# Layer 0's bias keys in the score products: two products of 260 columns in place of one of 512 and a separate path

## The chip, the cores and the metric

The kernel runs on one core of a Trainium2 chip. Its time is the device time of one execution in microseconds; the lower, the better. TensorE is called PE here, VectorE DVE, ScalarE ACT, GpSimd POOL, and SP is the engine that issues the DMAs. PEld is the loading of stationary weights into PE.

## The reference

The reference is a stack of four cross-attention layers on x (4 batches of 512 tokens, 512 wide) with a context of 64 tokens in each batch. The change is in layer 0. It has two attentions, one after the other, with 16 heads of 128 columns and one learned bias key and bias value for each head, and then an MLP. In short:

```python
h = layer_norm(x, ln_scale, ln_offset)
qh = (h @ wq + bq).reshape(b, 512, 16, 128)
kh = (ctx @ wk + bk).reshape(b, 64, 16, 128)
kh = concat([kh, broadcast(bias_k)], axis=1)        # 65 keys for each head
vh = concat([vh, broadcast(bias_v)], axis=1)
w = softmax(einsum("bqhk,bthk->bhqt", qh, kh) / sqrt(128))
x = x + einsum("bhqt,bthk->bqhk", w, vh).reshape(b, 512, 2048) @ wo + bo
```

Each query row has 65 scores for each head: 64 of the context, and one of the bias key. The bias key is the same in all batches. Everything is in fp32.

## The kernel before

**Algebra.** The kernel never forms the queries. `l0_project` multiplies each head's key matrix by its query weights once: `A[c]` (c is one of NC = 4 blocks of 128 rows of the model width) holds wq times the keys of a head, so that scores are h times A. `cq` holds what the query bias adds. `U` holds values times output weights. A head's row in `A` and `cq` is KW = 260 columns: 4 batches of 64 keys, and then four equal columns for the bias key. The keys of a head come into the tile `kT`: an evacuation from PSUM that adds the key bias (`shift`, on ACT or DVE) writes 256 columns, and a small POOL copy (L718) writes the bias key into the last four. L729 is the product for A (260 columns), L735 that for cq, L748 and L761 those for U and the bias values.

**Loops.** Each of the two attentions (n) does its 16 heads in two halves of HH = 8. For each half, `l0_project` is called, and then `l0_attention` for each of the 4 batches b. Inside, t goes over NT = 4 tiles of 128 query rows. So there are 16 calls of `l0_attention` and 64 tiles. The normalised input, transposed, is `hT` (transposes L675, evacuated with scale and offset at L496 or L497).

**A call of `l0_attention` before the change.** First the scores of the bias keys for all 512 rows: four products (L793), each with 32 columns of `A[c]` as the stationary side, taken with a step of 65 through its 8 rows, and `hT[c]` as the moving side; each writes its own 32 partitions of one bank. The result is copied to SBUF (`sbT`). Four small products with `fold` (L802) add up the four blocks and turn the result around, and a DVE add (L807) with a column of cq gives `last`: for each row of each tile, the 8 scores of the bias keys. Then for each tile:

- the scores of the context: `mm4` (L634), four accumulating products of 512 columns (8 heads of 64) into one PSUM bank `p`
- DVE adds cq (L825) into `s3`, 8 heads of 65, and copies the 8 scores of `last` (L827) into the 65th places
- maximum (L830), subtraction (L832), exp on ACT (L834), sum (L837), reciprocal (L839)
- POOL multiplies by the reciprocal (L842, L844), PE transposes (L853), DVE or ACT copies
- the output product `mm4` with U (L634 too), and a DVE add into x (L861).

L634 is the line of the helper `mm4`; all its users stand under it, and the shapes tell them apart. L926 is the product of the MLPs, which take up most of the kernel after layer 0's attention; L885 is their additions on DVE or POOL.

**Order.** The order is not written by hand. Each `with pe(...)`, `dve(...)`, `either(...)` records an operation with an assumed cost. `Plan.order` then plays the program through with those costs, engine by engine: an engine takes the earliest recorded operation whose inputs are there and whose buffers fit, within a distance `AHEAD`. So operations of several tiles and of the next projection lie between one another. The result is a fixed order on each engine; waits are semaphores. PSUM is `Memory(1024, 4)`: four blocks of two banks (512 fp32 columns each), which can be split; `ps()` takes one bank, `ps(2)` a block. A tile's buffer comes free in the plan when its last user is done.

Of the kernel before, what the change touches and what calls it, by code (L numbers as in the profile page):

```python
# [14 lines left out]
ALU = mybir.AluOpType  # L15
# [3 lines left out]
P = 128  # L19
B = 4  # L20
S = 512
D = 512
T = 64
NT = S // P
NC = D // P
H = 16
HH = H // 2
DH = 32
KW = B * T + 4
F = 2048  # L30
LOWEST = -3.4028234663852886e38

# [164 lines left out]
class Plan:  # L197
# [19 lines left out]
    def sb(self, n):  # L217
        return Buf(self.sbuf, n)

    def ps(self, banks=1):  # L220
        return Buf(self.psum, 512 * banks)
# [308 lines left out]
def t_dve(n):  # L530
    return 0.15 + n * 0.00105


def t_act(n):
    return 0.19 + n * 0.00083
# [5 lines left out]

MM = {512: 0.859, KW: 0.438, 256: 0.432}
TR = 0.109
ROWS = 1.08
# [14 lines left out]
def stack(nc, const, sbuf, psum, a, out):  # L559
# [6 lines left out]
    fold = const.tile([P, P], FP, name="fold")  # L566
# [27 lines left out]
    sb, ps = pl.sb, pl.ps  # L594

    def col(name, i=None):
        lo, hi = _COL_AT[name]
        return cols[:, lo:hi] if i is None else cols[:, lo + i : lo + i + 1]


    def pe(us):
        return pl.op(PE=us)

    def dve(n):
        return pl.op(DVE=t_dve(n))
# [4 lines left out]
    def pool(n):  # L610
        return pl.op(POOL=t_pool(n))

    def either(n):
        return pl.op(ACT=t_act(n), DVE=t_dve(n))
# [5 lines left out]
    def loaded(src, *sizes):  # L620

        n = math.prod(sizes)
        t = sb(n)
        load(t.v(*sizes), src, n)
        return t

    def chunks(w):

        return w.rearrange("(c p) n -> p c n", p=P)

    def mm4(o, dst, lhs, rhs):

        for c in range(NC):
            o.matmul(dst, lhs(c), rhs(c), start=(c == 0), stop=(c == NC - 1))  # L634
# [53 lines left out]
    def l0_project(n, half):  # L688
        A = [sb(HH * KW) for _ in range(NC)]
        cq = sb(HH * KW)  # L690
        U = [sb(HH // 2 * D) for _ in range(B)]
        if not half:

            bvd = sb(H * DH)
            with pool(512) as o:
                o.memset(bvd.v(), 0.0)
            for g in range(4):
                with pool(4) as o:
                    o.tensor_copy(
                        bvd[:, g * 129 : g * 129 + 109 : 36], col(f"L0_xattn_bias_v{n}")[:, 4 * g : 4 * g + 4]  # L700
                    )
            bias[n] = [bvd, sb(D), None]
        bvd, ub, _ = bias[n]
        vTs, wos = [], []
        for j in range(HH):
            h = half * HH + j
            heads = slice(h * P, (h + 1) * P)

            wk = loaded(chunks(a[f"L0_wk{n}"][:, heads]), NC, P)
            wq = loaded(a[f"L0_wqT{n}"][heads, :], D)  # L710
            kT = sb(KW)
            p = ps()
            with pe(4 * MM[256]) as o:
                mm4(o, p[:, : B * T], lambda c: wk.v(NC, P)[:, c, :], lambda c: ctxT[:, c, :])
            with either(256) as o:
                o.shift(kT[:, : B * T].k(0), p[:, : B * T], col(f"L0_xattn_bk{n}", h))
            with pool(1) as o:
                o.tensor_copy(kT[:, B * T :].k(1), col(f"L0_xattn_bias_k{n}", h).to_broadcast([P, 4]))  # L718
            wv = loaded(chunks(a[f"L0_wv{n}"][:, heads]), NC, P)
            vT = sb(B * T)  # L720
            p = ps()
            with pe(4 * MM[256]) as o:
                mm4(o, p[:, : B * T], lambda c: wv.v(NC, P)[:, c, :], lambda c: ctxT[:, c, :])
            with either(256) as o:
                o.shift(vT.v(), p[:, : B * T], col(f"L0_xattn_bv{n}", h))
            for c in range(NC):
                p = ps()
                with pe(MM[KW]) as o:
                    o.matmul(p[:, :KW], wq[:, c * P : (c + 1) * P], kT.v(), start=True, stop=True)  # L729
                with either(KW) as o:  # L730
                    o.move(A[c].v(HH, KW)[:, j, :].k(j), p[:, :KW])

            p = ps()
            with pe(MM[KW]) as o:
                o.matmul(  # L735
                    p[:, :KW], col(f"L0_xattn_bq{n}", h).to_broadcast([P, P]), kT.v(), start=True, stop=True
                )
            with either(KW) as o:
                o.move(cq.v(HH, KW)[:, j, :].k(j), p[:, :KW])
            wo = loaded(a[f"L0_wo{n}"][heads, :], D)  # L740
            vTs.append(vT)
            wos.append(wo)
            if j % 2:
                for b in range(B):
                    p = ps()
                    with pe(PAIR) as o:
                        for e in range(2):
                            o.matmul(  # L748
                                p[e * T : (e + 1) * T, :],
                                vTs[j - 1 + e][:, b * T : (b + 1) * T],  # L750
                                wos[j - 1 + e].v(),
                                start=True,
                                stop=True,
                            )
                    with either(D) as o:
                        o.move(U[b].v(HH // 2, D)[:, j // 2, :].k(j // 2), p.v())
            if j % 4 == 3:
                p = ps()
                with pe(ROWS) as o:
                    for i in range(4):  # L760
                        o.matmul(  # L761
                            p[i * DH : (i + 1) * DH, :],
                            bvd.v(H, DH)[:, h - 3 + i, :],
                            wos[j - 3 + i].v(),
                            start=True,
                            stop=True,
                        )
                if h == 3:
                    with either(D) as o:
                        o.move(ub.v(), p.v())  # L770
                else:
                    with dve(D) as o:
                        o.tensor_tensor(ub.v(), p.v(), ub.v(), ALU.add)
        if half:

            ubr = sb(D)
            p = ps()
            with pe(MM[512]) as o:
                o.matmul(p.v(), fold, ub.v(), start=True, stop=True)
            with either(D) as o:  # L780
                o.move(ubr.v(), p.v())
            bias[n][2] = ubr
        return A, cq, U

    def l0_attention(n, half, b, hT, proj, pb):
        qs = 1.0 / math.sqrt(P)
        A, cq, U = proj


        p = ps()  # L790
        with pe(ROWS) as o:
            for c in range(NC):
                o.matmul(  # L793
                    p[c * DH : (c + 1) * DH, :], A[c][:, KW // 4 - 1 :: KW // 4], hT[c].v(), start=True, stop=True
                )
        sbT = sb(S)
        with either(S) as o:
            o.move(sbT.v(), p.v())
        p = ps()
        with pe(8 * TR) as o:  # L800
            for t in range(NT):
                o.matmul(  # L802
                    p[:, t * HH : (t + 1) * HH], sbT[:, t * P : (t + 1) * P], fold[:, 3:DH:4], start=True, stop=True
                )
        last = sb(NT * HH)
        with dve(32) as o:
            o.tensor_tensor(  # L807
                last.v(NT, HH),
                p[:, : NT * HH].split(NT, HH),
                cq.v(HH, KW)[:, :, B * T].new(1).bc(P, NT, HH),  # L810
                ALU.add,
            )
        for t in range(NT):
            p = ps()
            with pe(4 * MM[512]) as o:
                mm4(
                    o,
                    p.v(HH, T),
                    lambda c: hT[c][:, t * P : (t + 1) * P],
                    lambda c: A[c].v(HH, KW)[:, :, b * T : (b + 1) * T],  # L820
                )
            sc = sb(HH * (T + 1))
            s3 = sc.v(HH, T + 1)
            with dve(512) as o:
                o.tensor_tensor(s3[:, :, :T].k(0), p.v(HH, T), cq.v(HH, KW)[:, :, b * T : (b + 1) * T], ALU.add)  # L825
            with dve(8) as o:
                o.tensor_copy(s3[:, :, T].k(1), last.v(NT, HH)[:, t, :])  # L827
            m = sb(HH)
            with dve(520) as o:
                o.tensor_reduce(m.v(), s3, AX.X, ALU.max)  # L830
# [19 lines left out]
            p = ps()  # L850
# [6 lines left out]
            p = ps()  # L857
# [4 lines left out]
        if half:  # L862

            p = ps()
# [643 lines left out]
    for n in (1, 2):  # L1508
        hT, pb = [], []
# [16 lines left out]
    h = {}  # L1526
# [106 lines left out]
```

## Time and profile before

| | |
|---|---|
| median of 3 runs | 2876.68 us (2876.4 to 2878.92) |
| profiled execution | 2877.63 us |
| its span, first to last instruction | 2875.8 us |
| mean granted PE clock | 0.993 |
| PE busy | 2799.8 us, 97% of the span |
| DVE busy | 1841.8 us, 64% |
| ACT busy, POOL busy | 812.1 us (28%), 903.8 us (31%) |
| DMA | 129.58 MB, 45 GB/s in the mean |
| first product of an MLP (L926) | 810.11 us from the start |

The profile is of one execution. Matmuls are pipelined, and the ends of their records are modelled, so "busy" of PE is the time that some matmul record covers. The mean of a group is how long one record lasted, not how far apart two of them are. Each fp32 product of the program is two records on PE, and two weight loads. A group of instructions shows the line, the engine, the tiles written and read, the count, busy time, the mean of one in ns, and the idle time of the engine just before, with what ended it.

### The profile page before, as it was taken

The numbers are of one execution on the slowest core, as the hardware profiler recorded it, in microseconds if no ns is written. First come the engines' busy times: TensorE is split into PE (matmuls) and PEld (weight loads), VectorE is DVE, ScalarE is ACT, GpSimd is POOL, SyncE is SP. The second block draws the span as 40 slices with busy tenths as digits, with TensorE's granted clock in tenths as the row PEclk, the third lists the DMA queues.
The fourth block names the chain that finished last, engine by engine and source line by source line (L and its number), as shares of the span: only waits on it lengthen the run. The fifth ranks groups of instructions, "written<-read, shape, count | busy, mean of one in ns | idle before, by whom it ended". The sixth has DMA issues, their size and how long they took to land. (4 is left out here: it accounts for less than half of the span.)

```text
span 2875.8 us, 29017 instructions
## 1 busy us (share of the span) xinstructions
PE 2799.8 (97%) x10284; PEld 1421.3 (49%) x10284; DVE 1841.8 (64%) x3207; ACT 812.1 (28%) x1472; POOL 903.8 (31%) x847
## 2 busy tenths in 40 slices
PE   8999999999999999999999999999999998999999
PEld 6456455465455444454545445444444443444444
DVE  5646655555754475765667667476776677667655
ACT  1210111201231113543453345155432314232211
POOL 2530222501441251123113112212444456344531
PEclk9999999999999999999999999999999999999999
DMA  5112021120111220011112001201101020112110
GB/s 165 34 40 78 2 79 34 36 79 3 33 55 44 62 66 23 12 47 39 30 37 77 1 23 37 74 16 30 59 30 44 30 88 15 38 36 74 59 44 29
DMA packets 131023, 129.58 MB, mean 45 GB/s; under 512 B 6800, under 2 KB 105744, under 8 KB 130880
## 3 DMA queue, kind: packets, MB, share of 16 engines
q1 hardware_dynamic: 130512, 127.43, 14.1%
q8 instruction: 82, 1.34, 0.2%
q14 instruction: 61, 0.50, 0.1%
q0 software_dynamic: 80, 0.16, 0.0%
q10 hardware_dynamic: 288, 0.15, 0.0%
HBM read 123.52 MB, written 4.19 MB: 44 GB/s over the span
## 5 line engine op out<-in xcount | busy, mean ns | idle before, releaser
L926 PE MATMUL banks<-arena 128*128 128x512 f32 x2688 | 1213.7, 598 | 19.7 <-ACT arena L1336 6.8
L634 PE MATMUL banks<-arena 128*128 128x512 f32 (+2 forms) x1968 | 825.7, 570 | 1.3 <-ACT arena L487 1.0
L926 PEld LDWEIGHTS banks<-arena 128*128 128x128 f32 x2688 | 499.0, 191 | 618.3 <-issue 534.4
L885 POOL TENSOR_TENSOR arena<-arena 128x512 f32<-128x512 f32 x292 | 420.9, 1448 | 656.4 <-DVE arena L488 184.9
L634 PEld LDWEIGHTS banks<-arena 128*128 128x128 f32 x1968 | 358.6, 190 | 418.1 <-issue 395.4
L488 DVE COPY arena<-banks 128x512 f32<-128x512 f32 (+3 forms) x538 | 313.9, 589 | 184.4 <-PE banks L926 64.7
L487 ACT COPY arena<-banks 128x512 f32<-128x512 f32 (+3 forms) x370 | 192.9, 542 | 576.0 <-PE banks L926 185.3
L885 DVE TENSOR_TENSOR arena<-arena 128x512 f32<-128x512 f32 x320 | 310.9, 980 | 65.4 <-ACT arena L960 22.4
L960 ACT ACTIVATE arena<-arena,cols 128x512 f32<-128x512 f32 x192 | 137.8, 721 | 452.6 <-DVE arena L885 218.3
L945 DVE TENSOR_TENSOR arena<-banks,arena 128x512 f32<-128x512 f32 x240 | 164.4, 687 | 122.2 <-PE banks L926 113.7
L1336 ACT ACTIVATE arena<-banks,arena 128x512 f32<-128x512 f32 x256 | 174.5, 687 | 118.6 <-DVE arena L1326 63.7
L842 POOL TENSOR_TENSOR arena<-arena 128x512 f32<-128x512 f32 x64 | 71.5, 1117 | 416.8 <-DVE arena L839 381.4
L1324 DVE TENSOR_REDUCE arena<-banks 128x1 f32<-128x512 f32 x256 | 168.0, 682 | 12.5 <-PE banks L1313 11.6
L493 DVE TENSOR_SCALAR arena<-banks,cols 128x256 f32<-128x256 f32 (+1 forms) x103 | 59.6, 579 | 171.5 <-PE banks L634 166.2
L634 PE MATMUL banks<-ctxT,arena 128*128 128x256 f32 x640 | 150.5, 386 | 10.1 <-DMA arena<-in_L_wk 7.7
L1370 PEld LDWEIGHTS banks<-ident,arena 128*128 128x128 f32 x1024 | 119.5, 144 | 81.0 <-ACT arena L1336 33.9
L1370 PE MATMUL banks<-ident,arena 128*128 128x128 f32 x1024 | 140.2, 281 | 10.2 <-ACT arena L1336 8.8
L634 PEld LDWEIGHTS banks<-ctxT,arena 128*128 128x128 f32 x640 | 120.7, 192 | 44.0 <-issue 13.2
L984 DVE TENSOR_TENSOR arena<-banks,arena 128x512 f32<-128x512 f32 x144 | 98.5, 687 | 67.2 <-PE banks L926 66.8
L834 ACT ACTIVATE arena<-arena 128x520 f32<-128x520 f32 x64 | 40.8, 637 | 325.5 <-DVE arena L832 319.7
L1347 POOL TENSOR_TENSOR arena<-arena 128x256 f32<-128x256 f32 x64 | 40.2, 628 | 285.8 <-DVE arena L1326 171.3
L666 POOL TENSOR_SCALAR arena<-arena 128x512 f32<-128x512 f32 x48 | 100.5, 2101 | 48.3 <-DVE arena L661 34.7
(147 smaller groups left out, 2369.8 us busy)
## 6 DMA issues: line engine op xcount, KB each, us to landing
arena<-in_L_w SPq DMA_DIRECT2D x192, 256.0 KB, 3.7
arena<-in_L_wk SPq DMA_DIRECT2D x48, 256.0 KB, 3.3
arena<-in_L_wqT SPq DMA_DIRECT2D x32, 256.0 KB, 4.3
arena<-in_L_wv SPq DMA_DIRECT2D x32, 256.0 KB, 4.4
arena<-in_L_wo SPq DMA_DIRECT2D x32, 256.0 KB, 3.5
arena<-in_L_wo SPq DMA_DIRECT2D x8, 1024.0 KB, 5.4
arena<-in_L_wv SPq DMA_DIRECT2D x6, 1024.0 KB, 8.6
arena<-in_L_wq SPq DMA_DIRECT2D x5, 1024.0 KB, 8.5
```

The lines of the kernel that those rows point to most:

```text
L487: "ACT": lambda e, out, in_: e.copy(out, in_),
L488: "DVE": lambda e, out, in_: e.tensor_copy(out, in_),
L634: o.matmul(dst, lhs(c), rhs(c), start=(c == 0), stop=(c == NC - 1))
L666: o.tensor_scalar(n.v(), src[t].v(), mv.v(NT, 2)[:, t, 0:1], rstd[:, t : t + 1], ALU.subtract, ALU.mult)
L885: o.tensor_tensor(out, x, y, op)
L926: o.matmul(p.v(), lhs(c, m), rhs(c), start=(c == 0), stop=(c == 1))
L945: o.tensor_tensor(t.v(), p.v(), y.v(), ALU.add)
L960: o.activation(g[f].v(), src.v(), func, bias=col(b1, q * NC + f))
L984: o.tensor_tensor(r.v(), p.v(), r.v(), ALU.add)
L1324: o.tensor_reduce(m[:, i : i + 1].k(i), banks[i].v(), AX.X, ALU.max)
L1336: o.activation(y.v(), banks[i].v(), AF.Exp, bias=nm[:, i : i + 1].k(i), scale=qs, accum_out=sums[:, i : i + 1].k(i),)
L1370: o.transpose(p[:, c * P : (c + 1) * P], e[i][:, c * P : (c + 1) * P], ident)
```

## The change

A head's row stays at KW = 260 columns, but is laid out as 4 batches of 65: 64 keys and the bias key as the 65th. The shift into `kT` writes four runs of 64 with a step of 65, and the POOL copy writes the 65th columns. In `l0_attention` the path of the bias keys (L793, `sbT`, L802, L807, L827) is gone. The scores of a tile have 8 x 65 = 520 columns, which is more than one bank of 512. They are made by two `mm4` of 260 columns, four heads each, into the two banks of a `ps(2)`; the stationary blocks of `hT` are loaded for each of the two. One DVE add takes all 520 columns from both banks.

```diff
-KW = B * T + 4
+KW = B * (T + 1)
...
-                o.shift(kT[:, : B * T].k(0), p[:, : B * T], col(f"L0_xattn_bk{n}", h))
+                o.shift(kT.v(B, T + 1)[:, :, :T].k(0), p[:, : B * T].split(B, T), col(f"L0_xattn_bk{n}", h))
             with pool(1) as o:
-                o.tensor_copy(kT[:, B * T :].k(1), col(f"L0_xattn_bias_k{n}", h).to_broadcast([P, 4]))
+                o.tensor_copy(kT.v(B, T + 1)[:, :, T].k(1), col(f"L0_xattn_bias_k{n}", h).to_broadcast([P, B]))
...
-        p = ps()
-        with pe(ROWS) as o:
-            for c in range(NC):
-                o.matmul(
-                    p[c * DH : (c + 1) * DH, :], A[c][:, KW // 4 - 1 :: KW // 4], hT[c].v(), start=True, stop=True
-                )
-        sbT = sb(S)
-        with either(S) as o:
-            o.move(sbT.v(), p.v())
-        p = ps()
-        with pe(8 * TR) as o:
-            for t in range(NT):
-                o.matmul(
-                    p[:, t * HH : (t + 1) * HH], sbT[:, t * P : (t + 1) * P], fold[:, 3:DH:4], start=True, stop=True
-                )
-        last = sb(NT * HH)
-        with dve(32) as o:
-            o.tensor_tensor(
-                last.v(NT, HH),
-                p[:, : NT * HH].split(NT, HH),
-                cq.v(HH, KW)[:, :, B * T].new(1).bc(P, NT, HH),
-                ALU.add,
-            )
         for t in range(NT):
-            p = ps()
-            with pe(4 * MM[512]) as o:
-                mm4(
-                    o,
-                    p.v(HH, T),
-                    lambda c: hT[c][:, t * P : (t + 1) * P],
-                    lambda c: A[c].v(HH, KW)[:, :, b * T : (b + 1) * T],
-                )
+            p = ps(2)
+            own = slice(b * (T + 1), (b + 1) * (T + 1))
+            with pe(8 * MM[KW]) as o:
+                for i in range(2):
+                    mm4(
+                        o,
+                        p.v(2, 512)[:, i, :KW],
+                        lambda c: hT[c][:, t * P : (t + 1) * P],
+                        lambda c: A[c].v(HH, KW)[:, 4 * i : 4 * i + 4, own],
+                    )
             sc = sb(HH * (T + 1))
             s3 = sc.v(HH, T + 1)
-            with dve(512) as o:
-                o.tensor_tensor(s3[:, :, :T].k(0), p.v(HH, T), cq.v(HH, KW)[:, :, b * T : (b + 1) * T], ALU.add)
-            with dve(8) as o:
-                o.tensor_copy(s3[:, :, T].k(1), last.v(NT, HH)[:, t, :])
+            with dve(520) as o:
+                o.tensor_tensor(
+                    sc.v(2, 4, T + 1),
+                    p.v(2, 512)[:, :, :KW].arrange("p i (h s) -> p i h s", h=4),
+                    cq.v(2, 4, KW)[:, :, :, own],
+                    ALU.add,
+                )
```

## The prediction

> **What bounds the kernel now.** I read the page's first two parts, then busy time by window, the groups by shape, and last the order of PE in time, with the start of each run of matmuls. The page's busy times first:
>
> ```profile
> PE 2799.8 (97%) x10284; PEld 1421.3 (49%) x10284; DVE 1841.8 (64%) x3207; ACT 812.1 (28%) x1472; POOL 903.8 (31%) x847
> ```
>
> PE is the only engine near full, but this is an average over stages, so I ask for the stage of the change. Layer 0's attention runs from about 76 us, and the first product of the MLP after it (L926) starts at 810.11 us. Windows in it (us; busy time of PE, PEld, DVE, ACT, POOL):
>
> ```profile
> 100.00:175.00 75.00, 75.00 (x258) 37.84 (x256) 42.96 (x82) 18.14 (x28) 37.51 (x35) 1.00 0.03 8
> 270.00:330.00 60.00, 60.00 (x201) 27.81 (x194) 34.59 (x66) 9.00 (x15) 10.97 (x16) 1.00 0.00 1
> 475.00:525.00 50.00, 47.37 (x162) 23.89 (x161) 32.23 (x68) 15.72 (x24) 33.30 (x38) 1.00 0.00 1
> 675.00:750.00 75.00, 75.00 (x242) 34.62 (x241) 46.52 (x92) 13.03 (x22) 14.02 (x20) 1.00 0.00 1
> ```
>
> PE has no gap in three of four, DVE has 40% to spare, the granted clock is full, and DMA is nearly still. Only at the start of the second attention (475 to 525) is PE short of work, by 2.6 us. So a microsecond of PE work taken out here is a microsecond off the end, as long as no one else becomes late. The groups concerned (count, busy us, mean ns of one):
>
> ```profile
> L634 PE MATMUL banks<-arena 128*128 128x512 f32 x1808 | 803.3, 594 | 1.0 <-ACT arena L487 1.0
> L729 PE MATMUL banks<-arena 128*128 128x260 f32 x256 | 61.8, 383 | 0.0
> L793 PE MATMUL banks<-arena 128*32 128x512 f32 x128 | 17.5, 617 | 3.7 <-DVE arena L497 2.1 <-ACT arena L496 1.6
> L802 PE MATMUL banks<-fold,arena 128*128 128x8 f32 x128 | 15.3, 246 | 0.0
> L827 DVE COPY arena<-arena 128x8 f32<-128x8 f32 x64 | 16.3, 289 | 13.0 <-PE banks L634 12.5
> ```
>
> Each matmul of the program is two records here (L729 is 128 matmuls and x256). The means are latencies: 256 x 383 ns is 98 us, not 61.8. Even busy over count (241 ns for 260 columns, 444 for 512) has the tail of each run in it, and short runs have more tail. So I price from starts. PE in order of time (start, length, records):
>
> ```profile
> 173.74 0.60 PE L853 MATMUL banks<-ident,arena 128*128 128x128 f32 x4
> 174.27 1.09 PE L793 MATMUL banks<-arena 128*32 128x512 f32 x8
> 175.30 3.70 PE L634 MATMUL banks<-arena 128*128 128x512 f32 x8
> 178.83 0.95 PE L802 MATMUL banks<-fold,arena 128*128 128x8 f32 x8
> 179.64 10.55 PE L634 MATMUL banks<-arena 128*128 128x512 f32 x24
> 190.03 0.60 PE L853 MATMUL banks<-ident,arena 128*128 128x128 f32 x4
> 190.46 7.03 PE L634 MATMUL banks<-arena 128*128 128x512 f32 x16
> 197.33 1.04 PE L853 MATMUL banks<-ident,arena 128*128 128x128 f32 x8
> ...
> 226.44 1.92 PE L729 MATMUL banks<-arena 128*128 128x260 f32 x8
> 228.19 0.60 PE L735 MATMUL banks<-arena,cols 128*128 128x260 f32 x2
> ```
>
> From one start to the next: 512 columns, (197.33 - 190.46) / 16 = 0.4294 us a record; 260 columns, (228.19 - 226.44) / 8 = 0.219. One L793 group takes 175.30 - 174.27 = 1.03 us, one L802 group 179.64 - 178.83 = 0.81. And the full-array run behind each of them is slow by a little: 3.53 us for 8 records where 3.43 is usual, 10.39 for 24 where 10.30 is.
>
> [...] L802, with only 8 columns to stream, runs at 101 ns a record[...]. A load therefore fits under a 219 ns record, as L729 shows with its own load before each. [...]
>
> **The change part by part.**
>
> 1. Gone: 16 L793 groups and 16 L802 groups. Summed start to start over all 16, 16.4 + 13.0 = 29.4 us of PE.
> 2. Gone with them: the slow first record behind each, about 0.10 us after 14 of the L793 groups and 0.08 after some 14 of the L802 groups: 2.5 us.
> 3. Score products: 64 tiles, each 16 records of 260 columns for 8 of 512: 16 x 0.2193 - 8 x 0.4293 = 0.075 us, x64 = 4.8 us more. This is the price of loading each weight block twice and of 8 more columns. Both lie in the 219 ns.
> 4. Other engines, all beside PE: DVE loses 64 copies (busy 16.3 us), 16 adds L807 (3.3) and, with ACT, 16 moves of sbT (0.69 each on DVE, 11); the score add grows from 512 to 520 columns, 64 x 0.011 = 0.7. About 30 us come off, net; worth nothing by itself, since DVE sits at 60%. If DVE were the bound, this would be a gain too.
> 5. The layout in the projection: the shift writes 4 runs of 64 instead of one of 256, and POOL's small copy (L718, median some 0.18 us) writes with a step. Same counts, same columns. I take zero; they lie under PE's own products of the next head. If the strided write cost 0.1 us, 32 shifts would be 3.2 us on an engine at 60%, covered.
> 6. Score tiles of two banks. A tile holds a quarter of PSUM from its first product to the end of the DVE add. By the order of PE in the changed program, often four score tiles stand in a row, which is all eight banks. The cover: a tile is 3.51 (scores) + 0.50 (transposes) + 3.43 (output) = 7.44 us on PE. In before, the adds L825 of tiles 2 to 4 started 0.3 to 0.9 us after their products (window from 76 us), so a block is back some 1.6 us after its last product, long before the fourth tile behind wants it. I take zero, at most 16 bursts x 0.5 = 8 us.
> 7. What stays: PE waits of 1.07, 0.99 and 1.62 us before the first L793 of a batch were for the normalised hT, which the first score product needs as well. They stay, so I count no gain from them. They could grow by 1 to 2 us at each of four starts, as PE now comes there earlier.
> 8. The order behind: from the first L926 on, PE's instructions are the same with a few swaps, SP's order is the same throughout, and 12 adds of L885 go from DVE to POOL (1448 ns each, 17 us of an engine at 31%). One or two ACT table loads more (1283 ns) lie on an engine at 28%. I take zero, give or take 3 us. All the DMAs keep their counts and order.
>
> Sum: -29.4 - 2.5 + 4.8 = -27.1 us. The span 2875.8 becomes 2848.7; the profiled execution, 2877.63 with what lies around the span, becomes 2850.5; it stood 0.95 us above the median, 2876.68, so I expect **2849.6 us**.
>
> For the unknown read of 65-column runs: 512 matmuls x 2 records. [...] The runs of 64 with jumps between them, in before, show no loss against whole rows (both 429 ns), so I take zero.
>
> **Rivals.**
>
> The gain is partly eaten: [...]waits for hT or for a block (up to 8). For it speaks that DVE is at 19.4 of 25 us where each of the two attentions starts, against it the covers above. Half to all of one of these gives 2853 to 2858; I give it 0.2, with 2855.
>
> The busy column was right: a 260-column record costs 241 ns and a 512 one 444, so 64 x (16 x 0.241 - 8 x 0.444) = 19.5 us more, against 32.8 busy us gone: -13, 2863. Against it, 219 is seen wherever L729 runs. 0.03.
>
> PSUM becomes the bound, and it ends slower: PE waits for a free pair of banks before each score tile, and as it runs in order, the transposes and output products behind wait too, and DVE's residual adds for them. The price is the 0.9 us that an add can be late, 64 x 0.9 = 57.6 us, less 27.1: 2907. It decides from 27.1 / 64 = 0.42 us per tile. For it, four tiles in a row fill PSUM; against it, 7.44 us of PE work per tile and DVE at 60%. 0.03.
>
> The change doing nothing would need the records of L793 and L802 to lie under other work; they don't, one follows the other on PE without a gap. 0.01.
>
> **How the numbers follow.** The likeliest case (0.73) is 2849.6, with 2846 to 2853 from item 8. Reaching to the eaten cases, the range is 2845 to 2859. A measurement can tell about 0.2% (5.8 us) from no change: faster holds the first three cases, 0.96; same 0.01; slower 0.03.
>
> **What would show it.** Right: the L793 and L802 rows gone; score runs at 219 ns a record from start to start, 3.51 us a tile; first L926 near 783 us; PE's idle time before it unchanged within 2 us. Wrong: score records at 226 ns or more[...], PE waits released by DVE's score add before a score product (PSUM), or idle time that grows behind 783 us.

## The result, and the profile after

The changed kernel takes 2855.24 us (median of 6 runs, 2853.82 to 2857.5) against 2877.52 us of the kernel before on the same chip (6 runs, 2876.4 to 2879.05). The ratio is 0.9923, with a 95% interval of 0.991 to 0.9935, so it is faster by 22.3 us. The forecast was 2849.6, a gain of 27.1 us on the runs that it was made from.

The busy times of the page after, in the same order as before (engine, us, share, instructions), and four windows in layer 0's attention (us; PE, PEld, DVE, ACT, POOL, clock, DMA share, GB/s):

```profile
PE 2772.7 (97%) x10540; PEld 1499.2 (53%) x10540; DVE 1817.4 (64%) x3102; ACT 814.2 (29%) x1471; POOL 916.0 (32%) x859
```

```profile
100.00:175.00 75.00, 75.00 (x301) 50.77 (x300) 36.95 (x66) 19.48 (x29) 39.40 (x37) 1.00 0.17 49
270.00:330.00 60.00, 60.00 (x241) 40.82 (x240) 31.91 (x54) 10.99 (x20) 10.46 (x16) 1.00 0.02 5
455.00:505.00 50.00, 48.61 (x200) 34.59 (x200) 35.52 (x64) 14.85 (x21) 47.20 (x43) 1.00 0.00 1
650.00:725.00 75.00, 75.00 (x299) 49.88 (x298) 48.06 (x90) 16.35 (x26) 22.25 (x26) 1.00 0.00 1
```

PE is still without a gap in three of four windows, and the start of the second attention waits 1.4 us where it waited 2.6. More loads of weights (PEld 50.77 for 37.84 in the first window) lie under the products: PE's busy time has no gap for them. The groups by shape, and PE in order of time at the start of the second half of the first attention:

```profile
L634 PE MATMUL banks<-arena 128*128 128x512 f32 x1296 | 577.5, 593 | 0.2 <-DVE arena L488 0.2
L634 PE MATMUL banks<-arena 128*128 128x260 f32 x1024 | 232.8, 381 | 2.2 <-ACT arena L496 1.1 <-DVE arena L497 1.1
```

```profile
270.08 7.18 PE L634 MATMUL banks<-arena 128*128 128x260 f32 x32
277.10 0.60 PE L834 MATMUL banks<-ident,arena 128*128 128x128 f32 x4
277.54 7.11 PE L634 MATMUL banks<-arena 128*128 128x260 f32 x24
284.48 1.04 PE L834 MATMUL banks<-ident,arena 128*128 128x128 f32 x8
```

The rows of L793 and L802 are gone, 1024 records of 260 columns stand for 512 of 512, and from 270.08 to 277.10 they come at (277.10 - 270.08) / 32 = 0.219 us each. Over all 976 neighbouring pairs of them the median spacing is 0.219. (The run of 24 from 277.54 mixes 16 of these with 8 records of 512, since a row shows the form of its first.) Who PE waited for in layer 0's attention after 60 us (us in total, times, longest):

```profile
PE banks L634 <- ACT arena L496: 1.1, 1, 1.1
PE banks L634 <- DVE arena L497: 1.1, 1, 1.1
PE banks L634 <- DVE arena L488: 0.2, 1, 0.2
```

No row names the score add (L803). Two-bank score tiles did not hold PE up, and the two waits left are those for hT.

**Where the 22.3 us are.** I split the time from the first matmul to the start of the last MLP product at the first MLP product, which is 810.11 us from the start in before and 780.25 after. In each part I add up the gaps between matmul records ("idle"), and half of the time for which the trace's clock entries grant PE only half its clock ("half clock"). Half, because in such stretches products of 512 columns stand 0.853 us apart in place of 0.429. The rest I call work. All figures of this kind are of the one profiled execution of each kernel.

| us | layer 0's attention: all = idle + half clock + work | behind it: all = idle + half clock + work |
|---|---|---|
| before | 802.4 = 6.1 + 0 + 796.3 | 2055.8 = 56.7 + 18.8 + 1980.3 |
| after | 772.4 = 3.0 + 0 + 769.4 | 2062.8 = 64.0 + 17.1 + 1981.8 |
| difference | -30.0, of it work -26.9 | +7.0, of it idle +7.3 |

So the part that was changed gave 30.0, more than forecast, and the part that was not changed took 7.0 back. The granted clock did not take it: half clock is 1.7 us less in after. Followed from one MLP product to the same one in the other trace, the distance is -29.8 us at 1080 us of the kernel before, -26.9 near 1540, -25.9 near 1870 and -22.3 near 1980. These stretches are layer 2's attention beside the MLPs. There PE waited for (before, then after, windows 1080 to 2100 and 1050 to 2077 us):

```profile
PE banks L1370 <- ACT arena L1336: 8.8, 9, 2.4
PE banks L1313 <- ACT arena L1336: 7.5, 7, 2.2
PE banks L926 <- ACT arena L1336: 6.8, 6, 2.7
```

```profile
PE banks L1351 <- ACT arena L1317: 11.7, 9, 2.5
PE banks L1294 <- ACT arena L1317: 9.9, 8, 2.3
PE banks L907 <- ACT arena L1317: 5.8, 4, 2.7
```

The lines are 19 lower after, the instructions are the same: transposes, scores of layer 2 and MLP products behind the exponentials on ACT. These waits have grown by 4.3 us in sum, out of 7.3 us of idle time.

### The profile page after: what moved, and what is told of

It is laid out like the page before. It is cut to its first block, busy times and chain, and to the rows that moved or that the text cites. A ratio compares the mean times of both kernels' runs of the same rounds, so it can differ in the third digit from the quotient of the medians.

```text
span 2853.2 us, 29411 instructions
## 1 busy us (share of the span) xinstructions
PE 2772.7 (97%) x10540; PEld 1499.2 (53%) x10540; DVE 1817.4 (64%) x3102; ACT 814.2 (29%) x1471; POOL 916.0 (32%) x859
## 5 line engine op out<-in xcount | busy, mean ns | idle before, releaser
L634 PE MATMUL banks<-arena 128*128 128x260 f32 (+3 forms) x2480 | 825.9, 486 | 2.7 <-ACT arena L496 1.1
L907 PEld LDWEIGHTS banks<-arena 128*128 128x128 f32 x2688 | 497.6, 190 | 615.4 <-issue 528.3
L866 POOL TENSOR_TENSOR arena<-arena 128x512 f32<-128x512 f32 x304 | 437.1, 1445 | 678.1 <-DVE arena L488 173.3
L634 PEld LDWEIGHTS banks<-arena 128*128 128x128 f32 x2480 | 454.6, 189 | 329.3 <-issue 287.2
L488 DVE COPY arena<-banks 128x512 f32<-128x512 f32 (+3 forms) x526 | 305.4, 586 | 180.9 <-PE banks L907 66.3
L487 ACT COPY arena<-banks 128x512 f32<-128x512 f32 (+2 forms) x366 | 190.8, 542 | 710.5 <-PE banks L907 191.1
L866 DVE TENSOR_TENSOR arena<-arena 128x512 f32<-128x512 f32 x308 | 302.7, 989 | 69.2 <-ACT arena L941 26.3
L926 DVE TENSOR_TENSOR arena<-banks,arena 128x512 f32<-128x512 f32 x240 | 163.9, 686 | 131.1 <-PE banks L907 120.7
L823 POOL TENSOR_TENSOR arena<-arena 128x512 f32<-128x512 f32 x64 | 72.0, 1125 | 397.1 <-DVE arena L820 355.9
L1351 PE MATMUL banks<-ident,arena 128*128 128x128 f32 x1024 | 141.0, 283 | 13.3 <-ACT arena L1317 11.7
L965 DVE TENSOR_TENSOR arena<-banks,arena 128x512 f32<-128x512 f32 x144 | 98.2, 685 | 65.1 <-PE banks L907 65.0
L842 DVE TENSOR_TENSOR arena<-banks,arena 128x512 f32<-128x512 f32 x64 | 44.1, 690 | 94.5 <-PE banks L634 94.3
```

What stands on the lines that cost most here:

```text
L487: "ACT": lambda e, out, in_: e.copy(out, in_),
L488: "DVE": lambda e, out, in_: e.tensor_copy(out, in_),
L866: o.tensor_tensor(out, x, y, op)
L907: o.matmul(p.v(), lhs(c, m), rhs(c), start=(c == 0), stop=(c == 1))
L926: o.tensor_tensor(t.v(), p.v(), y.v(), ALU.add)
L965: o.tensor_tensor(r.v(), p.v(), r.v(), ALU.add)
```

## The experiments

Two questions were left: what took the 7 us back, and whether the parts of the sum are right. **Theory A**: the planner plays the whole program through, so a shorter layer 0 gives it another state behind, and it makes another order there, with other waits. **Rival B**: the new layer 0 itself slows what is behind. All ratios are to the kernel before on the same chip.

**1 and 2. The order behind, held.** The sequence in which the planner begins the operations behind layer 0, with their engines, was written out from one kernel and played in the other. Inside layer 0 the planner works as ever, and each engine takes an operation of the list only when it has none of layer 0:

```diff
         def arm(op):
+            if op.n >= self.seam:
+                armed.add(op.n)
+                return
...
+                    if choice is None and head < len(queue) and queue[head][1] == e:
+                        op = self.ops[self.seam + queue[head][0]]
+                        if op.n in armed and op.ready <= now + 1e-9 and op.pos <= limit + self.ahead:
...
+                                choice = op
+                                head += 1
```

> The changed kernel, but every operation behind layer 0's attention stands on the engine and in the order that the kernel before gives it; layer 0's attention itself is ordered as in the changed kernel. Theory A (the 7 us given back between 1080 and 2000 us come from the order behind, which the planner set anew): -30 us against before, 2847 to 2848; the distance to before stays at -30 from the first MLP product to the end. Rival B (something in the changed layer 0 itself makes the part behind slower, such as the granted clock or where its buffers lie): 2855 as the changed kernel. In between would mean both.

Measured: 2853.78 us, ratio 0.9919 (0.9905 to 0.9932).

> The kernel before, but every operation behind layer 0's attention stands on the engine and in the order that the changed kernel gives it. Theory A: slower than before by the 7 us, 2884 to 2885, lost between 1080 and 2000 us. Rival B: 2877 to 2878, as before.

Measured: 2893.52 us, ratio 1.0055 (1.0042 to 1.0069).

Experiment 1 lies within 1.3 us of rival B's number and not at theory A's; experiment 2 lies beyond both, 9 us above A's. Nor did layer 0 stay as it was: it is 774.9 us long in experiment 1, 2.5 more than in the changed kernel, and 806.8 in experiment 2, 4.5 more than in before. Operations of the part behind lie between those of layer 0, so that holding their order changes layer 0 too. Neither run isolates the order behind. Idle and half clock behind layer 0, in one table with those of experiments 3 and 4, which hold the order of before as well:

| idle + half clock behind, us | order behind of before | order behind of after |
|---|---|---|
| bias path kept | 75.5 (before), 76.2 (exp. 4) | 85.3 (exp. 2) |
| bias path gone | 78.6 (exp. 1), 74.5 (exp. 3) | 81.1 (after) |

Down a column the two layers 0 differ by no fixed sign; across a row, the new order waits longer by 2.5 to 9.8 us, as one pairs the figures. In time behind layer 0, before has 2055.8, after 2062.8, experiment 1 2060.4 and experiment 2 2067.4. If an exchange of orders costs the same in both directions, that is 7.0 us for the order, 4.6 for the exchange (other buffers, another seam) and 0.0 for the layer 0. The last is worked out, on that assumption. On it these runs speak for A; without it they leave B open, since with the old order behind the new layer 0 has 4.6 us more there. Two runs don't settle it.

**3 and 4. One part alone.** In experiment 3 the path is gone and nothing is in its place; in 4 it is kept and the products are split, and one DVE add reads both banks. Both have the order of before behind. The excerpts show the core of each.

```diff
...
-                o.tensor_copy(s3[:, :, T].k(1), last.v(NT, HH)[:, t, :])
+                o.tensor_copy(s3[:, :, T].k(1), cq.v(HH, KW)[:, :, B * T])
```

```diff
-            p = ps()
-            with pe(4 * MM[512]) as o:
-                mm4(o, p.v(HH, T), ..., lambda c: A[c].v(HH, KW)[:, :, b * T : (b + 1) * T])
+            p = ps(2)
+            own = slice(b * T, (b + 1) * T)
+            with pe(8 * MM[KW]) as o:
+                for i in range(2):
+                    mm4(o, p.v(2, 512)[:, i, : 4 * T], ..., lambda c: A[c].v(HH, KW)[:, 4 * i : 4 * i + 4, own])
...
```

> The kernel before without the separate path of the bias keys, and nothing in its place: the four L793 products, the copy sbT, the L802 products and the add are left out, and the 65th score of a head is the entry of cq alone, so the scores of the bias keys lack their product with h. The order behind layer 0's attention is that of before. My sum: 29.4 us of products and 2.5 us of slow first records off PE, -31.9, so 2845 to 2846, or up to 3 us less where PE's waits in layer 0 shrink too, as they did in the changed kernel (5.5 to 3.5 us and 1.5 to 0.5). Rival: part of the path lay beside other products, and the path alone is worth only some 20 us: 2857.

Measured: 2862.05 us, ratio 0.9948 (0.9936 to 0.9961), a gain of 14.7 only.

> The kernel before with its separate path of the bias keys kept and its layout of 64 columns a head kept, but the scores made by two products of 256 columns into two banks for one of 512. The order behind layer 0's attention is that of before. My sum: 64 x (16 x 0.2158 - 8 x 0.4293) = +1.2 us, 2878 to 2879, give or take 2 for PE's waits in layer 0. Rival (two-bank score tiles run PSUM short): PE waits on DVE's score add before score products, +5 us or more, 2883 and up.

Measured: 2900.14 us, ratio 1.0075 (1.0062 to 1.0087), a loss of 23.4. For the 0.2158 of the sum, the trace of before has 0.216 us from one start to the next (median of its records of 256 columns).

As times both miss. The account tells why: in layer 0, experiment 3 has work 765.3 (31.0 less than before, forecast 31.9), but 18.3 idle for 6.1, and 5.1 of half clock. Experiment 4 has work 800.6 (some 4 more, forecast 1.2), idle 15.7 and half clock 8.5. Its PE in order of time, in the projection of the second half (its line 835 is L729, 841 is L735, 594 is L488):

```profile
244.72 0.60 PE L835 MATMUL banks<-arena 128*128 128x260 f32 x2
245.84 0.71 PE L835 MATMUL banks<-arena 128*128 128x260 f32 x2 [0.52 <-DVE arena L594]
247.06 0.71 PE L835 MATMUL banks<-arena 128*128 128x260 f32 x2 [0.52 <-DVE arena L594]
248.29 0.71 PE L835 MATMUL banks<-arena 128*128 128x260 f32 x2 [0.52 <-DVE arena L594]
```

One product is made, evacuated by DVE, and only then the next: 1.22 us from start to start for a product that takes 0.44 elsewhere. PE waits for room in PSUM here, in the projection, and not for the score add. My reading is that work started far ahead holds all SBUF blocks in this plan, so that values and U products sit in PSUM and can't be moved out; no trace shows which blocks are held, so this is argued only. Experiment 3, without any two-bank tile, has more idle time still. So the two tell roughly the work of each part, and that kernels with such small edits can lose some 17 us in idle time and half clock; they do not tell the time of each part.

**5 to 8. The four kernels in a calmer plan.** The same four (before, after, no path, path kept with two products), all with other settings of the planner and nothing else; no order is held.

```diff
-AHEAD, AHEAD_LOAD, RESERVE = 150.0, 60.0, 4
+AHEAD, AHEAD_LOAD, RESERVE = 120.0, 80.0, 2
```

> The kernel before with other settings of the planner alone: operations may run 120 us ahead instead of 150, loads 80 instead of 60, and 2 blocks of SBUF are held back instead of 4. The same operations, another order. Theory S (what a kernel waits is set by the plan, and not by the change of layer 0): PE's work, meaning the time that is neither idle nor at half clock, stays at 796 us in layer 0 and 1980 behind, and the waits (6 us in layer 0, 75 behind, half clock included) move by some 10 us either way; I expect fewer, 2860 to 2876. Rival: the waits are set by the data flow, and stay: 2877.

Measured: 2859.95 us, ratio 0.9946 (0.9932 to 0.9959). Work 796.4 in layer 0, the waits behind 53.6 for 75.5. That is at the lower end of the range of the theory in which waits are the plan's; that the data flow alone sets them does not hold. Work behind was expected to stay at 1980 and is 1987.0, so that work, as counted here, also moves with the plan by some us.

> The changed kernel with the same other settings of the planner (120, 80, 2). Theory S: work 769 us in layer 0 and 1981 behind as in the changed kernel, so 27 less than the kernel before with these settings, and up to 6 us either way for what the two plans wait; 2832 to 2850. This would beat both kernels. Rival (the changed layer 0 itself makes the part behind wait longer): the distance to before with the same settings stays at 22, with 7 more waits behind.

Measured: 2841.46 us, ratio 0.9872 (0.9858 to 0.9885). Layer 0 is 26.6 us shorter than in experiment 5, 25.5 of it work; the part behind is 10.1 us longer. 18.5 us in all, fewer than theory S allows: here the rival is nearer.

> The kernel before without the separate path of the bias keys (the scores of the bias keys then lack their product with h), with the same other settings of the planner. Against before with these settings: work -31 to -32 us in layer 0, none behind; time -32, up to 6 us either way for the waits. Rival (part of the path lay beside other products): -20 in work.

Measured: 2841.36 us, ratio 0.9874 (0.9861 to 0.9888). Work in layer 0 is 766.3, 30.1 less than in experiment 5. So the path stood in PE's way with nearly all of its 31.9, and the reading that part of it lay beside other products falls. The time missed its range: it is 18.6 us below experiment 5, where 26 to 38 were expected, as the part behind is 11.7 us longer, 11.6 of it waits and half clock.

> The kernel before with the separate path kept, and two products of 256 columns into two banks for one of 512, with the same other settings of the planner. Against before with these settings: work +1.2 us in layer 0 from 64 x (16 x 0.2158 - 8 x 0.4293), none behind; time +1, up to 6 us either way for the waits. Rival (two-bank tiles run PSUM short): waits for DVE's score add before score products in layer 0, +5 us and more there.

Measured: 2861.11 us, ratio 0.9941 (0.9929 to 0.9954), 1.2 us above experiment 5. Work in layer 0 is 799.6, 3.2 more than there, where 1.2 was forecast. The waits of PE in its layer 0, after 60 us:

```profile
PE banks L793 <- DVE arena L497: 1.1, 1, 1.1
PE banks L748 <- ACT arena L487: 0.4, 1, 0.4
PE banks L634 <- DVE arena L488: 0.3, 1, 0.3
```

Nothing waits for the score add. So two-bank tiles by themselves need not cost PE a wait. Whether they had a share in the shortage of experiment 4, whose plan is another, these runs don't tell.

**9 to 12. Two more settings,** since after two pairs the part behind was longer both times. Only the three numbers differ: 160, 80, 2 and 110, 80, 3.

> The kernel before with a third setting of the planner (operations may run 160 us ahead, loads 80, 2 blocks held back). Theory S (the waits behind layer 0 belong to each plan by chance): work 796 in layer 0; waits and half clock behind anywhere from 50 to 75 us; 2850 to 2875.

Measured: 2866.7 us, ratio 0.996 (0.9945 to 0.9975). Work is 795.9 in layer 0, waits and half clock behind 60.7, as expected.

> The changed kernel with the same third setting (160, 80, 2). Work -27 us in layer 0 against before with this setting, none behind: on this all theories agree. The waits and half clock behind, against before with this setting: theory S, anything from -10 to +10 us, with no sign that holds through the settings; rival (the shorter layer 0 makes the part behind wait, as in the two settings so far, +6 and +10): again +5 to +10.

Measured: 2835.84 us, ratio 0.9849 (0.9833 to 0.9866), 30.9 below experiment 9. Waits and half clock behind are 2.0 less than there, which the rival does not allow; work behind is 2.0 less too.

> The kernel before with a fourth setting of the planner (110, 80, 3). As for the third: work 796 in layer 0, waits and half clock behind 50 to 75 us, 2850 to 2875.

Measured: 2864.18 us, ratio 0.9954 (0.9939 to 0.9969). Waits and half clock behind are 59.8. Work in layer 0 is 792.3 and not 796: in this plan 32 transposes, 3.7 us of PE, stand behind the first MLP product that stand ahead of it in the other kernels of the four pairs.

> The changed kernel with the same fourth setting (110, 80, 3). Work -27 us in layer 0 against before with this setting. Waits and half clock behind against before with it: theory S, -10 to +10; rival, +5 to +10 again. If three or four of the four pairs stand at +5 to +10, the rival is the better reading.

Measured: 2835.23 us, ratio 0.9845 (0.983 to 0.986), 29.0 below experiment 11. With experiment 10 it is the fastest: both beat before and after. The profiled execution took 2827.01, 8.2 us less than the median, so what its trace shows behind layer 0 (waits and half clock 5.5 less than in experiment 11) is of a lucky one.

The four pairs side by side, after less before, each pair with the same settings. The third and fourth columns are of the profiled executions. The last is an estimate: the difference of the medians less that of layer 0, taking layer 0 to be the same in every execution.

| settings | medians, us | layer 0 (work) | part behind | behind, from medians |
|---|---|---|---|---|
| 150, 60, 4 (as given) | -22.3 | -30.0 (-26.9) | +7.0 | +7.7 |
| 120, 80, 2 | -18.5 | -26.6 (-25.5) | +10.1 | +8.1 |
| 160, 80, 2 | -30.9 | -26.4 (-25.9) | -4.0 | -4.4 |
| 110, 80, 3 | -29.0 | -26.4 (-25.4) | -9.4 | -2.5 |

Layer 0 gains 26 to 30 us in each, work 25.4 to 26.9. The fourth pair's -9.4 should not be leaned on: with the medians it is -2.5, and with the 32 transposes counted in layer 0 in both kernels about +1. So the part behind changes by some -4 to +8 us. Two pairs of four stand at +5 to +10 and two don't, so the rival of a steady loss behind falls. This is what theory A expects: the plan behind is made anew and comes out better or worse. That the order alone made the 7 us is not shown, since experiments 1 and 2 could not isolate it, and which of the swaps did it was not tried.

## Why the prediction was right, point by point

**Steps 1 to 3** (the path's 29.4, the slow first records 2.5, the split 4.8; -27.1 in sum) were right together: work in layer 0 fell by 26.9 here, and by 25.4 to 25.9 in the other pairs. That the first agrees within 0.2 us is luck in part. By work alone the parts fit less well: the path took 30.1 to 31.0 for 31.9, the split 3.2 for 1.2 in experiment 8. Both make the gain smaller, so they don't cancel.

The traces show where these us are, if one adds up the time from one start to the next, gaps left out, for each group of products in layer 0:

| us | forecast | measured |
|---|---|---|
| products of L793 and L802, gone (exp. 7 less 5) | -29.4 | -29.2 |
| score and output products, 512 columns (exp. 7 less 5) | -2.5 | -2.5 |
| score and output products, scores of 256 columns (exp. 8 less 5) | +1.2 | +1.4 |
| score and output products, scores of 260 columns (exp. 6 less 5) | -2.5 + 4.8 | +2.3 |

Each price was right. The 1.4 to 1.8 us by which the work of experiments 6 to 8 stands above their sums lie in products that the change left alone, most of them in the projections (the first products of keys and values from the context, and L729), which each plan puts between other neighbours.

**Prices from starts, not from busy time,** was the choice that mattered. Busy over count is still high for 260 columns after the change: 232.8 / 1024 = 0.227, and the rival that took 0.241 would have had 2863. The time measured lies between the two forecasts; it is the work in layer 0, -26.9 and not -13, that decides.

**Step 4** held: DVE's busy time fell by 24.4 us, and nothing of that size came of it, as PE stayed almost without gaps in both kernels. I had said about 30 with ACT's part in it. **Step 5** held: no wait for the shift or the copy appears.

**Step 6 and the slower rival** (PSUM): no PE wait for L803 in after, none for the score add in experiment 8. There was more cover than I had said: four score tiles stand in a row only 3 times, 40 of the 64 tiles stand alone, and at no time are more than two of them between their first product and the end of their add. What I had not seen is that PE can wait for room in PSUM in the projection (experiment 4, 0.52 us a product).

**The runs of 65 columns** cost nothing: 0.219 us a record in after, as in L729 with whole rows, and under the 226 ns that the prediction had named against itself. It had called the read an unknown and taken zero, and the trace decides against a price.

**Step 7** was mis-sized: I took no change in PE's idle time in layer 0, possibly more, and it fell by 3.1 us. Waits of 1.0, 0.72 and 1.62 us at the start of the second attention became one of 1.1 and two of 0.2 and less.

**Step 8** is the term that failed. I read PE's order behind as the same with a few swaps and took zero, give or take 3; it was +7.0, and the idle time that grew there by 7.3 is a sign that the prediction had named against itself. Of what it listed, 12 adds did go to POOL, six of them net in the stretch where the time was lost. The two more table loads both lie in layer 0; behind it both kernels have 80. PE waits for ACT in that stretch in before too, so a swap there can well lengthen a wait, but this is argued: no run shows which swap did it. The four pairs tell the size of the term for a replanned program, some -4 to +8 us where I had allowed 3.

**The number.** 2855.24 lies outside the 2846 to 2853 of the likeliest case and within the stated range. The eaten case had the right size (2855) with the wrong place: I had looked for the loss inside layer 0. So that the range holds is owed in part to a case whose reason did not come true.

## What to carry to other kernels

Price a matmul from one start to the next in a long run of its own shape; latencies and busy times of short runs both misled here (260 columns in after: 0.219 us from start to start, 0.381 as the mean of a record, 0.227 as busy over count). When an order is made by a planner, a change in one stage replans all that is behind: count a term of its own for that, sized by how much the same program moves under other settings (here the part behind of the unchanged kernel took 2041 to 2056 us under four), and don't set it to zero because few instructions moved. To learn what a part is worth, compare work and waits apart, and run the pair under several plans.

## What the runs showed of the hardware that was not expected

Some short gaps on PE came with a second cost beside the idle time, a slower PE. Up to the last MLP product, the clock entries grant half clock in seven stretches of before and eight of after, of 3.41 us or two or three times that; each begins between 0.9 us before and 2.0 us after the end of a gap of more than 1 us. That the gap brings the half clock is my reading: no run changed a gap alone. After the gap of 2.69 us that ends at 1256.5 us in before, half clock stands for 3.41 us from 1257.8 (PE in order of time, then a window: busy time of PE, PEld, DVE, ACT and POOL, granted clock, DMA share, GB/s):

```profile
1256.54 2.60 PE L926 MATMUL banks<-arena 128*128 128x512 f32 x4 [2.69 <-ACT arena L1336]
```

```profile
1257.80:1261.20 3.40, 3.40 (x13) 2.51 (x12) 1.73 (x6) 1.32 (x5) 0.00 (x0) 0.50 0.00 0
```

Transposes inside stand 0.213 us apart, where they stand 0.109 apart at full clock. The length of a gap alone does not decide: in after, half clock follows a gap of 1.78 us, and none follows one of 2.33. It also follows several short gaps: in experiment 4, four gaps of 0.52 us, one every 1.2 us from 245.3 us on, are followed by 10.2 us of half clock. Behind layer 0 these stretches cost 18.8 us in before, 17.1 after, and 5.1 in the profiled execution of experiment 12. The mean granted clock differs from one execution to the next of the same kernel. The core views of experiments 12 and 6 (span, mean granted clock):

```profile
core 0: 2825.2 us, clock 0.998
```

```profile
core 0: 2841.5 us, clock 0.995
```

Experiment 12's other executions ran at 0.996 and took 2834 to 2836 us, its profiled one 2827; experiment 6 had one at 0.997 with 2836.92 us among 2841 to 2843 at 0.995 and 0.996. So a single execution is good to some 5 to 9 us here, and the medians should be compared.
